# A message-passing layer on one core: the sums of a group made eight times side by side in place of four

## The chip, the cores and the metric

The kernel runs on one core of one Trainium2 chip. The metric is the device time of one execution in microseconds. A core has TensorE (PE, with its weight loads PEld), VectorE (DVE), ScalarE (ACT), GpSimd (POOL) and SyncE (SP), each with a queue of its own, and 16 DMA engines.

## The reference

The layer has 12500 nodes with 64 features and 212500 edges with 32 features, everything in float32. The edges are sorted by their target node.

```python
msg_in = concatenate([nodes[row], nodes[col], edge_features], axis=-1)
messages = relu(msg_in @ mW1 + mb1) @ mW2 + mb2
aggregated = segment_sum(messages, col, num_segments=12500)
upd_in = concatenate([nodes, aggregated], axis=-1)
u = relu(upd_in @ uW1 + ub1) @ uW2 + ub2
out = layernorm(nodes + u)          # over the 64 features, no scale
```

The hidden layer has 128 units. The kernel sums the hidden units over the edges of a node first and applies `mW2`, folded into the update's weights, afterwards.

## The kernel before, in words

**Groups.** The edges are cut into 554 groups (`G`) of three tiles of 128 edges. As they are sorted, the targets of a group lie in a window of 32 nodes (`W`). A group passes through three parts.

- `turn` (L318, L326): three gathers (`gather`, L132, indirect DMAs issued by POOL, 128 rows of 64 features each) have put the source nodes' rows beside a one-hot matrix of the edges' places in the window, which VectorE makes (L306), in one of 20 buffers `own_s`. PE transposes the three tiles (L318) and ACT copies them, 96 rows by 384 columns, into `own_st` (L326), where a DMA by SP has put the edge features. The copy also counts the edges of each node.
- `hidden` (L339, L349): three matmuls of `own_st` with the group's weights `own_wm` make the hidden units before relu, and ACT writes relu of them to `own_h`. Thirty-two rows of `own_wm` are the window's target nodes times their weights; they are made for four groups at a time (L285, L292, L297).
- `sums` (L363, L365): one small transpose brings the counts into a row. Three matmuls, one for each tile, have the hidden units as the stationary operand and the one-hot matrix as the moving one, and accumulate in PSUM the sums of the hidden units for each of the 32 nodes. VectorE adds them to `agg` (L374) and the counts to a row of `xc` (L375), at the window's place.

**The copies of the sums.** The one-hot matrix has 32 columns. The kernel before repeats it `TIMES` = 4 times along the moving operand with a broadcast, so that a matmul has 128 columns, and the sums stand four times side by side in the PSUM bank. Only the first copy is read.

**Steps.** One loop over `k` writes out the order for all engines. For the first 544 values a step on PE is the transposes of group k, the hidden units of group k - 2 and the sums of group k - 4, one after another, and only the last matmul of a step tells that it is done. Everything that follows the step waits for that: the copy L326, relu L349, the adds L374 and L375. Two sets of PSUM banks alternate between the steps, so a step waits for what read the step two before. VectorE makes the one-hot of group k + 1 before the adds of step k in its queue. For the last ten groups (`SHORT`) every part is a step of its own, and the sums of groups 540 to 543 already fall into that part.

**Gathers.** The gathers of group k + 16 stand in POOL's queue after step k. A gather waits until the copy L326 of the group 20 before it has read its buffer.

**Update.** Every 512 nodes whose edges are done are updated between the steps (L392 to L426): two matmuls with 512 columns, relu, four matmuls, the layer norm and a store.

If the edges were not sorted a second program would run; it does not run here.

Of the kernel before, what the change touches and what calls it, by code (L numbers as in the profile page):

```python
# [28 lines left out]
W = 32  # L29
TG = 3  # L30
GE = TG * P
G = (E + GE - 1) // GE
# [10 lines left out]
BITS = 16  # L43
NEAR_GROUPS = 24
SHORT = 10
TIMES = 4


def tiles_of(g):

    n = min(GE, E - g * GE)
    return [min(P, n - j * P) for j in range((n + P - 1) // P)]
# [43 lines left out]
def ordered(ctx: ExitStack, tc: tile.TileContext, a, own, ok):  # L96
# [21 lines left out]
    def after(first, *others):  # L118

        tc.declare_no_dep(first.ins, group="quiet", reason="waits for the last of a step")  # L120
        for i in others:
            tc.add_manual_dep(
                first.ins, i.ins.name,
                mybir.DependencyInfo(mybir.DependencyClass.Sync, mybir.DependencyReason.DATA),
                reason="the kernel's own rings",
            )
        return first
# [160 lines left out]
    def windows(b, wp, own_bank=True):  # L288


        xw, n = xws.pop(b)
        did = nc.tensor.matmul(wp[: n * W, :], xw[:, :n, :], w1b, start=True, stop=True)  # L292

        def copies():
            for i in range(n):
                g = b * SB + i
                c = nc.vector.tensor_copy(wm[g % NW][:W, :], wp[i * W : (i + 1) * W, :])  # L297
                after(c, *([did] if own_bank else []), *([hidden_by[g - NW]] if g >= NW else []))
                wm_by[g] = c

        return did, copies
# [57 lines left out]
    def sums(g, ps):  # L359
        h, s = own.h[g % NH], own.s[g % RING]  # L360
        sizes = tiles_of(g)
        sg = ps[:, 2, : (TIMES + 1) * W].rearrange("p (t w) -> p t w", w=W)
        did = [nc.tensor.transpose(sg[0:1, TIMES, :], counts[:W, g : g + 1], ident[:W, :W])]  # L363
        for j, p in enumerate(sizes):
            did.append(nc.tensor.matmul(  # L365
                sg[:, :TIMES, :], h[:p, j, :],
                s[:p, j, :W].unsqueeze(1).to_broadcast([p, TIMES, W]),
                start=j == 0, stop=j == len(sizes) - 1))

        def add(step):  # L370
            sums_by[g] = step
            at = bass.ds(starts.pop(g), W)
            return [
                after(nc.vector.tensor_tensor(agg[:, at], sg[:, 0, :], agg[:, at], ALU.add), step),  # L374
                after(nc.vector.tensor_tensor(xc[0:1, at], sg[0:1, TIMES, :], xc[0:1, at],  # L375
                                              ALU.add), step),
            ]

        return did, [*relu_by[g], copy_by[g]], add
# [53 lines left out]
    def step_update(g):  # L433
# [5 lines left out]
        elif now:  # L439
            got = now[1](now[0])  # L440
            now = [got, *now[2:]] if len(now) > 2 else []

    users = {part: [[], []] for part in (turn, hidden, sums)}

    def step(*work):
# [10 lines left out]
        for part, g, *_ in parts:  # L456
            if part is sums:
                for b in [b for b in xws if (b - 1) * SB <= g][:1]:
                    last, copies = windows(b, own.ps[g % 2][:, 2, (TIMES + 1) * W :][:, :H])
                    did.append(last)  # L460
# [18 lines left out]
    for k in range(G):  # L479
        if k < BITS:  # L480
            bit(k)
        if k % SB == 2:
            inputs(k // SB + 2)
        if k % SB == 1:
            places(k // SB + 1)
        onehot(k + 1)
        if k < G - SHORT:
            step((turn, k), *([(hidden, k - 2)] if k > 1 else []),
                 *([(sums, k - 4)] if k > 3 else []))
            made, summed = max(0, k - 1), max(0, k - 3)  # L490
        else:

            step((turn, k))
            for _ in range(2):
                if summed < made:
                    step((sums, summed))
                    summed += 1
            for _ in range(2):
                if made <= k:
                    step((hidden, made))  # L500
                    made += 1
        if k + AHEAD < G:
            gather(k + AHEAD)
# [332 lines left out]
```

## Time and profile before

| | |
|---|---|
| median of 8 runs | 2565.02 us (2561.79 to 2568.23) |
| the profiled execution | 2563.38 us |
| its span, first to last instruction | 2561.7 us |
| mean granted clock of TensorE | 0.771 of full speed |
| busy: PE, PEld, POOL | 1652.9, 1434.5, 1574.3 us |
| busy: DVE, ACT | 572.4, 542.0 us |
| granted clock, tenths, 40 slices | 9577777777877777877777877877777778777778 |

An engine's busy time counts each moment once, however many of its instructions overlap. The clock of a slice is the mean of what the throttle granted. "Idle before" is the time that an engine stood still ahead of a group of instructions, with what ended it. The chain is followed back from the last instruction, at each step to what released it.

### The profile page before, as it was taken

Reading aid. Unit: us, or ns where it says so; the run is one execution under the profiler, and the core shown is the slowest. Engines: PE = TensorE matmul, PEld = TensorE weight load, DVE = VectorE, ACT = ScalarE, POOL = GpSimd, SP = SyncE. Lnnn points to the kernel's source line nnn. Section 1 sums busy time; section 2 is a strip of 40 time slices with the busy share of each in tenths; the row PEclk is TensorE's granted clock in tenths of the full one; section 3 lists DMA queues with packets and bytes.
Section 4 is the critical chain, followed back from the end, with each engine's and each line's share of the span. In section 5 each row is a group of like instructions: output and inputs, shape, how many; then the busy total and the mean of one; then the engine's idle time right before and its main releaser. Section 6 shows DMA issues by size and latency. Waiting matters only on the chain.

```text
span 2561.7 us, 30668 instructions
## 1 busy us (share of the span) xinstructions
PE 1652.9 (65%) x9441; PEld 1434.5 (56%) x9441; DVE 572.4 (22%) x3191; ACT 542.0 (21%) x1715; POOL 1574.3 (61%) x1668
## 2 busy tenths in 40 slices
PE   1366666666676666766666666756667676666667
PEld 0355555555565555655565555655556565655565
DVE  4012122221221221222212222222222122122222
ACT  0122222222222222222222222222222222222222
POOL 7566666666666666666666666666666666666650
PEclk9577777777877877777877877778777878777778
DMA  4221111111111111111111111111111111111110
GB/s 89 45 48 39 34 37 36 35 36 38 34 39 32 39 39 31 39 34 37 39 34 37 36 35 36 37 37 36 38 34 39 32 39 39 32 36 37 36 36 12
DMA packets 73364, 96.05 MB, mean 37 GB/s; under 512 B 33451, under 2 KB 40842, under 8 KB 73194
## 3 DMA queue, kind: packets, MB, share of 16 engines
q0 software_dynamic: 53152, 54.51, 12.2%
q1 hardware_dynamic: 19128, 39.03, 5.4%
q8 instruction: 80, 1.31, 0.2%
q14 instruction: 90, 0.74, 0.1%
q10 hardware_dynamic: 914, 0.46, 0.1%
HBM read 90.58 MB, written 3.20 MB: 37 GB/s over the span
## 4 chain that ended last, share of the span: by engine, by line
PE 43%; another core or an unknown queue 31%; issue 14%; ACT 9%; DVE 2%; DMA 0%; DVEq 0%; SPq 0%; ACTq 0%
PE own_ps L365 17%; PE own_ps L339 12%; PE own_ps L318 7%; ACT own_st L326 5%; ACT own_h L349 5%; PE own_ps L363 2%; PE own_ps L292 1%; PE u_ps L405 1%; PE u_ps L392 1%; PE u_ps L393 1%; DVE mv L412 0%; DVE stats L411 0%; DMA dlc_i<-in_dst_cols 0%; DVE own_wm L297 0%
## 5 line engine op out<-in xcount | busy, mean ns | idle before, releaser
L132 POOL DMA_INDIRECT own_s<-in_x,src_sb x1661 | 1573.5, 947 | 912.4 <-issue 538.9
L318 PE MATMUL own_ps<-own_ident,own_s 128*96 128x128 f32 x1661 | 363.0, 340 | 792.8 <-issue 435.4
L318 PEld LDWEIGHTS own_ps<-own_ident,own_s 128*96 128x96 f32 x1661 | 227.4, 158 | 865.4 <-issue 477.0
L326 ACT ACTIVATE own_st<-own_ps 96x384 f32<-96x384 f32 x554 | 268.8, 485 | 1878.4 <-remote 873.3
L365 PE MATMUL own_ps<-own_s,own_h 128*128 128x128 f32 x3322 | 652.9, 345 | 3.2 <-issue 3.2
L339 PE MATMUL own_ps<-own_wm,own_st 128*128 128x128 f32 x3322 | 610.0, 335 | 1.2 <-DVE own_wm L297 1.2
L339 PEld LDWEIGHTS own_ps<-own_wm,own_st 128*128 128x128 f32 x3322 | 565.7, 251 | 4.7 <-DVE own_wm L297 1.6
L365 PEld LDWEIGHTS own_ps<-own_s,own_h 128*128 128x128 f32 x3322 | 530.5, 238 | 29.8 <-issue 2.5
L374 DVE TENSOR_TENSOR agg<-own_ps,agg 128x32 f32 x554 | 106.0, 191 | 1842.7 <-ACT own_h L349 1229.5
L349 ACT ACTIVATE own_h<-own_ps 128x384 f32<-128x384 f32 x553 | 264.2, 478 | 17.0 <-PE own_ps L339 13.1
L297 DVE COPY own_wm<-own_ps 32x128 f32<-32x128 f32 x550 | 155.1, 282 | 7.0 <-issue 1.0
L306 DVE TENSOR_TENSOR own_s<-iota,dlc 128x96 f32<-128x96 f32 x554 | 133.0, 241 | 4.7 <-issue 0.6
L363 PE MATMUL own_ps<-own_ident,own_counts 32*1 32x32 f32 x554 | 107.0, 193 | 4.0 <-ACT own_st L326 1.9
L326 ACT ACTIVATION_READ_ACCUMULATOR own_st<-own_ps 96x1 f32 x554 | 106.7, 193 | 0.0
L375 DVE TENSOR_TENSOR xc<-own_ps,xc 1x32 f32 x554 | 99.1, 179 | 15.2 <-PE u_ps L393 6.4
L363 PEld LDWEIGHTS own_ps<-own_ident,own_counts 32*1 32x1 f32 x554 | 41.1, 74 | 94.7 <-issue 49.1
L405 PE MATMUL u_ps<-u,u 128*128 128x64 f32 (+1 forms) x196 | 49.9, 406 | 28.5 <-issue 15.4
L405 PEld LDWEIGHTS u_ps<-u,u 128*128 128x128 f32 (+1 forms) x196 | 47.1, 324 | 31.9 <-issue 16.3
L285 DVE COPY xw<-xc 66x32 f32 x554 | 60.4, 175 | 3.0 <-issue 2.4
L292 PE MATMUL own_ps<-w1b,xw 66*128 66x128 f32 (+1 forms) x276 | 58.6, 296 | 0.0
L392 PE MATMUL u_ps<-agg,wc 128*128 128x512 f32 (+1 forms) x50 | 36.4, 820 | 28.1 <-issue 17.1
L292 PEld LDWEIGHTS own_ps<-w1b,xw 66*128 66x128 f32 (+1 forms) x276 | 47.0, 213 | 0.1
(58 smaller groups left out, 202.0 us busy)
## 6 DMA issues: line engine op xcount, KB each, us to landing
own_s<-in_x,src_sb POOLq DMA_INDIRECT x1661
own_st<-in_efT SPq DMA_DIRECT2D x138, 192.0 KB
xin<-in_x SPq DMA_DIRECT2D x24, 128.0 KB
out<-o SPq DMA_DIRECT2D x24, 128.0 KB
xc<-in_xT SPq DMA_DIRECT2D x12, 179.2 KB
dlc_i<-in_dst_cols SPq DMA_DIRECT2D x1, 831.0 KB
xc<-in_xT SPq DMA_DIRECT2D x4, 179.5 KB
src_sb<-in_src SPq DMA_DIRECT2D x13, 50.5 KB
```

Source lines behind the costliest of these rows:

```text
L132: nc.gpsimd.indirect_dma_start(out=s[:p, j, W:], out_offset=None, in_=x[:, :], in_offset=bass.IndirectOffsetOnAxis(ap=src_sb[:p, g * TG + ...
L292: did = nc.tensor.matmul(wp[: n * W, :], xw[:, :n, :], w1b, start=True, stop=True)
L297: c = nc.vector.tensor_copy(wm[g % NW][:W, :], wp[i * W : (i + 1) * W, :])
L306: places_by[g] = nc.vector.tensor_tensor(own.s[g % RING][:, :, :W], iota.unsqueeze(1).to_broadcast([P, TG, W]), dlc[:, g * TG : (g + 1) * ...
L318: nc.tensor.transpose(xt[:, j * P : j * P + p], s[:p, j, :], ident[:p, :p])
L326: nc.scalar.activation(t[: D + W, c : c + n], xt[:, :n], AF.Copy, accum_out=counts[:, g : g + 1]), step)
L339: nc.tensor.matmul(pre[:p, j, :], t[:, c + j * P : c + j * P + p], wm[g % NW], start=True, stop=True)
L349: relu_by[g] = [nc.scalar.activation(h, pre, AF.Relu)]
L363: did = [nc.tensor.transpose(sg[0:1, TIMES, :], counts[:W, g : g + 1], ident[:W, :W])]
L365: did.append(nc.tensor.matmul(sg[:, :TIMES, :], h[:p, j, :], s[:p, j, :W].unsqueeze(1).to_broadcast([p, TIMES, W]), start=j == 0, stop=j = ...
L374: after(nc.vector.tensor_tensor(agg[:, at], sg[:, 0, :], agg[:, at], ALU.add), step),
L405: nc.tensor.matmul(o_ps[:p, k], u[:, k:q:n], u2, start=True, stop=True)
```

## The change

`TIMES` becomes 8: the moving operand of the sums' matmuls has 256 columns and the sums stand eight times side by side. The last ten groups keep four copies (`FEW`). The transposed counts now stand behind eight copies in the bank. The number and the order of instructions on every engine are the same.

```diff
-TIMES = 4
+TIMES = 8
+FEW = 4
...
         sg = ps[:, 2, : (TIMES + 1) * W].rearrange("p (t w) -> p t w", w=W)
+        times = TIMES if g < G - SHORT else FEW
         did = [nc.tensor.transpose(sg[0:1, TIMES, :], counts[:W, g : g + 1], ident[:W, :W])]
         for j, p in enumerate(sizes):
             did.append(nc.tensor.matmul(
-                sg[:, :TIMES, :], h[:p, j, :],
-                s[:p, j, :W].unsqueeze(1).to_broadcast([p, TIMES, W]),
+                sg[:, :times, :], h[:p, j, :],
+                s[:p, j, :W].unsqueeze(1).to_broadcast([p, times, W]),
                 start=j == 0, stop=j == len(sizes) - 1))
```

## The prediction

> **What bounds the kernel now.** I read the page's groups first, then the chain, the waits, the timeline of an ordinary stretch and of the stretch in which the gathers have stopped, and last two windows of different clock.
>
> ```profile
> PE 1652.9 (65%) x9441; PEld 1434.5 (56%) x9441; DVE 572.4 (22%) x3191; ACT 542.0 (21%) x1715; POOL 1574.3 (61%) x1668
> L132 POOL DMA_INDIRECT own_s<-in_x,src_sb x1661 | 1573.5, 947 | 912.4 <-issue 538.9
> L365 PE MATMUL own_ps<-own_s,own_h 128*128 128x128 f32 x3322 | 652.9, 345 | 3.2 <-issue 3.2
> ```
>
> No engine is full. The sums are L365: 1661 matmuls, three for each group of three tiles, with two records each. POOL works 0.947 us on a gather and starts the next 1.25 us after the last when nothing stops it, so 1661 gathers need 2076 us. The rest of POOL's idle time is waiting, above all for L326 (363.9 us in the view of waits), since a gather may fill a buffer only when the group 20 before it was copied.
>
> ```profile
> PE 43%; another core or an unknown queue 31%; issue 14%; ACT 9%; DVE 2%; DMA 0%; DVEq 0%; SPq 0%; ACTq 0%
> PE own_ps L365 17%; PE own_ps L339 12%; PE own_ps L318 7%; ACT own_st L326 5%; ACT own_h L349 5%; PE own_ps L363 2%; PE own_ps L292 1%; PE u_ps L405 1%; PE u_ps L392 1%; PE u_ps L393 1%; DVE mv L412 0%; DVE stats L411 0%; DMA dlc_i<-in_dst_cols 0%; DVE own_wm L297 0%
> ```
>
> The 31%, 794 us, are time that no record explains. The timeline shows what it is. L326 copies the transposes of one step, in order, and waits for the last matmul of that step.
>
> ```profile
> 1013.60 0.85 PE L318 MATMUL own_ps<-own_ident,own_s 128*96 128x128 f32 x3
> 1015.19 0.94 PE L365 MATMUL own_ps<-own_s,own_h 128*128 128x128 f32 x6
> 1015.96 0.49 PE L318 MATMUL own_ps<-own_ident,own_s 128*96 128x128 f32 x3
> 1019.70 0.49 ACT L326 ACTIVATE own_st<-own_ps 96x384 f32<-96x384 f32 x1 [4.90 <-PE own_ps L292]
> 1021.27 0.84 PE L318 MATMUL own_ps<-own_ident,own_s 128*96 128x128 f32 x3 [2.94 <-ACT own_h L349]
> ...
> 2493.05 0.49 PE L318 MATMUL own_ps<-own_ident,own_s 128*96 128x128 f32 x3
> 2494.26 0.94 PE L365 MATMUL own_ps<-own_s,own_h 128*128 128x128 f32 x6
> 2495.23 0.49 ACT L326 ACTIVATE own_st<-own_ps 96x384 f32<-96x384 f32 x1 [1.02 <-PE own_ps L365]
> ```
>
> The step that starts at 1013.60 has its last record end at 1016.13, but its copy starts at 1019.70, 3.6 us later, and PE's step after next (1021.27) starts only after that. The step at 2493.05 ends at 2495.20 and is copied at 2495.23. Between these, one thing differs: POOL's last gather starts at 2486.5. Matching the copies with the triples of L318 in order over groups 20 to 535, I count 3.1 us on average from a step's recorded end to its copy, and about one step in four with less than 0.1 us. So while gathers run, most steps are seen as finished long after PE's records end. What holds them back the trace does not name.
>
> ```profile
> 2200.00:2300.00 100.00, 67.73 (x376) 59.30 (x376) 21.64 (x125) 22.26 (x71) 62.49 (x67) 0.72 0.17 35
> 1400.00:1500.00 100.00, 65.27 (x380) 55.62 (x381) 22.98 (x132) 22.68 (x72) 62.66 (x67) 0.83 0.18 37
> 2493.00:2505.00 12.00, 10.51 (x84) 9.35 (x83) 4.55 (x26) 5.05 (x16) 0.00 (x0) 1.00 0.06 16
> 1000.00:1012.00 12.00, 5.91 (x36) 4.92 (x35) 2.79 (x17) 2.76 (x9) 7.18 (x8) 0.78 0.19 39
> ```
>
> The first two windows hold 67 gathers each, with a granted clock of 0.72 and of 0.83: a PE that is 15% quicker did not make the groups come quicker. The last two show how the clock goes with PE's work: 1.00 at 10.51 us busy of 12 (88%), 0.78 at 49%.
>
> **The change, part by part.** Sums: groups 0 to 543 get a moving operand of 256 columns in place of 128. That is 544 x 3 x 2 = 3264 records. What a record of more columns costs is read from starts. At half clock the two 512-column records of L393 take from 222.52 to 224.22, 0.85 us each, and the three 128-column records of L318 after them to 224.86, 0.213 each: four times the columns, four times the time. So 256 columns take 0.427 us at half clock and 0.213 at full clock, where 128 took 0.213 and 0.11. Added: 3264 x 0.107 = 349 us if the clock were always full, 3264 x 0.213 = 695 us if always half, and at the mean clock of 0.771 3264 x 0.139 = 453 us.
>
> Page "TensorE: Matmul & The Clock Gate", section "Back-to-back issue gap", of the Trainium skill gives 134 cycles for 128 columns and 262 for 256 when warm, which would add an estimated 174 us in 3264 records. The trace has two passes in each record (0.11 us, not 0.056), and by the rows it is 349.
>
> Nothing else moves: the order of instructions on every engine is the same, no wait is added, the bank holds it (9 x 32 columns and 128 for the windows, 416 of 512), VectorE still adds 32 columns from the first copy, and the transposed count only lies further along. The last ten groups keep 128 columns. But the sums of groups 540 to 543 are made in the last part, where no gathers run: 24 records x 0.107 = 2.6 us with nothing to cover them.
>
> Clock: PE's 1652.9 us at 0.771 become (1652.9 + 453) x 0.771 = 1624 us of full-clock work. Busy share b = 1624 / (2562 c), which is 0.634 / c. A straight line through (0.645, 0.771) and the end row (0.88, 1.00) gives c = 0.771 + 0.97 (b - 0.645). Both hold at about c = 0.86 (b = 0.74). This is an estimate; its bounds are no change (0.771) and 1.00.
>
> The same page, section on the HAM clock gate, has the clock as half or full only, half after a window of some 3.4 us of idleness. If eight copies left no such window, the clock would be 1.00.
>
> What lies on the path: on the chain the PE lines other than L365 have 22%, 564 us. At 0.86 they shrink by 564 x (1 - 0.771/0.862) = 60 us. Half of that I count as gained, since the two windows show that a quicker PE is largely swallowed by the late completions: -30 us. The sums' own growth, 453 us at the old clock, 0.83 us in a group, I count at nothing beyond the 2.6 us: it ends before the copy would have started in the three steps of four that wait 0.1 to 10 us. If that cover is gone it costs what the rivals below say. The sum against the profiled execution (2563.4 us; span 2561.7 and 1.7 around it): 2563.4 - 30 + 2.6 = 2536. The median of the runs is 1.6 us above the profiled one, so I say 2537.
>
> **Rivals.** *The cover is missing where it counts (slower).* The steps that complete at once, one in four, are where PE's end is the completion. There 136 groups each get 0.83 us later: +113, less 30: 2648. The place is the copy L326 after these steps, which POOL waits for; it decides when POOL has used up the gathers that earlier copies allow. A step early in a run of gathers has some 2.5 us to spare (two more gathers), a step at its end none. For it: all of the 363.9 us of POOL's waiting for L326. Against it: the two windows. At its worst completion follows PE's end in every step. Then L365's 435 us on the chain become 435 x 2 x 0.771/0.862 = 778, +343, less 60: 2848. A single decisive price inside this is the clock staying at 0.77, when a half-clock step grows from 3.84 us (1009.97 to 1013.81) to 5.12, over the 4.5 us that a group has.
>
> *Nothing to be seen.* All of PE's time is covered, the clock's gain too: 2563 + 2.6 - 2, within 0.2%.
>
> *A larger gain.* A steadier PE lets copies come before POOL has run dry. A third of POOL's wait for L326 gone is -121: 2444. For it: three quarters of the steps are not at PE's speed now, so their pattern may shift. Against it: nothing in the change touches the gathers.
>
> *The change is not made as told.* Left out: the built program has 544 groups with 256 columns and ten with 128.
>
> **How the numbers follow.** Forecast (hidden, clock up): 0.46 with the larger gain, of which 0.06 lies below 2450. No difference, within 0.2% (5 us, about what a measurement of this kernel tells from none): 0.10. Slower: 0.44, of which 0.32 lies up to 2720 and 0.12 above, towards 2848. The range 2450 to 2720 leaves out 0.18. The forecast's own range is 2500 to 2560. Both signs hold most of the chance, and the point is that of the likeliest single case.
>
> **What would show it.** L365 at 345 ns mean now: records of about 450 to 480 ns, PE busy near 75%, a clock near 0.86. Right, if the mean distance from a step's end to L326 shrinks by about what the steps grow, and POOL's wait for L326 does not grow. Wrong on the cover, if L326 waits for L365 longer with L365's chain share near 30%. Wrong on the clock, if it stays below 0.80. The stretch after the last gather should be 3 us longer.

## The result: 2572.4 us, slightly slower

| | before | after |
|---|---|---|
| median | 2564.2 us (33 runs) | 2572.4 us (12 runs) |
| ratio | | 1.0034, 95% interval 1.0027 to 1.0042 |
| the profiled execution, its span | 2563.4, 2561.7 us | 2573.9, 2572.1 us |
| mean granted clock | 0.771 | 0.874 |

The change costs 8 us by the medians. In the experiments further on, two single executions of the kernel before took 3002.7 and 3002.9 us, at a granted clock of 1.00, where the others took 2101 to 2108 us; they are left out of the ratios there. The page of the profiled execution after, with the line of busy times, the two lines of the chain, and the groups that the forecast speaks of (busy time, mean ns of one, idle time before them):

```profile
PE 1862.5 (72%) x9441; PEld 1505.4 (59%) x9441; DVE 572.9 (22%) x3191; ACT 543.6 (21%) x1715; POOL 1573.5 (61%) x1668
...
PE 49%; another core or an unknown queue 25%; issue 14%; ACT 9%; DVE 2%; DMA 0%; ACTq 0%; DVEq 0%
PE own_ps L367 26%; PE own_ps L340 11%; PE own_ps L319 6%; ACT own_h L350 4%; ACT own_st L327 4%; PE u_ps L407 2%; PE own_ps L365 2%; PE own_ps L293 1%; PE u_ps L394 1%; PE u_ps L395 1%; ACT u L397 0%; DMA u1s<-in_uW 0%; DVE own_wm L298 0%; DVE mv L414 0%
...
L133 POOL DMA_INDIRECT own_s<-in_x,src_sb x1661 | 1572.7, 947 | 918.8 <-issue 546.5
L367 PE MATMUL own_ps<-own_s,own_h 128*128 128x256 f32 (+1 forms) x3322 | 1001.7, 444 | 0.0
L319 PE MATMUL own_ps<-own_ident,own_s 128*96 128x128 f32 x1661 | 315.1, 304 | 605.7 <-issue 282.8
...
L340 PE MATMUL own_ps<-own_wm,own_st 128*128 128x128 f32 x3322 | 533.7, 304 | 0.6 <-DVE own_wm L298 0.6
```

The transposes and the hidden units in the page of before:

```profile
L318 PE MATMUL own_ps<-own_ident,own_s 128*96 128x128 f32 x1661 | 363.0, 340 | 792.8 <-issue 435.4
...
L339 PE MATMUL own_ps<-own_wm,own_st 128*128 128x128 f32 x3322 | 610.0, 335 | 1.2 <-DVE own_wm L297 1.2
```

The line numbers have moved by one up to L350, and the sums are L367. Read against before: PE worked 209.6 us longer, and the span is only 10.4 us longer. The sums grew by 348.8 us (652.9 to 1001.7). The hidden units shrank by 76.3 (L339 610.0, L340 533.7) and the transposes by 47.9 (363.0 to 315.1), although their number and shape are the same: they run at a higher clock. On the chain the sums rose from 17% to 26%, and the time that no record explains fell from 31% to 25%. POOL's work and its idle time are almost the same.

In the timeline after, one stretch with gathers and one behind the last gather, the steps of PE and their copies L327:

```profile
1000.45 0.49 PE L319 MATMUL own_ps<-own_ident,own_s 128*96 128x128 f32 x3
...
1001.66 1.56 PE L367 MATMUL own_ps<-own_s,own_h 128*128 128x256 f32 x6
...
1006.91 0.49 ACT L327 ACTIVATE own_st<-own_ps 96x384 f32<-96x384 f32 x1 [2.00 <-remote]
...
1007.09 0.51 PE L319 MATMUL own_ps<-own_ident,own_s 128*96 128x128 f32 x3 [3.87 <-issue]
...
2500.23 1.56 PE L367 MATMUL own_ps<-own_s,own_h 128*128 128x256 f32 x6
...
2501.83 0.49 ACT L327 ACTIVATE own_st<-own_ps 96x384 f32<-96x384 f32 x1 [1.65 <-PE own_ps L367]
```

The step that starts at 1000.45 ends at 1003.22, and its copy comes at 1006.91, 3.7 us later. Behind the last gather (2492.2) the sums end at 2501.79 and the copy comes 0.04 us later. So the late completions of before are still there. Counted over groups 20 to 535, in the same way as before, a step of PE lasts 3.29 us in place of 2.88, and the copy comes 2.51 us after its end in place of 3.09. From the start of a step to its copy it is 5.80 us in place of 5.97.

One more count from the two traces says what sets the pace. When the transposes of a group start, POOL has started the gathers of 18.4 groups more on average (18.4 after the change too), nearly the 20 that the ring holds. So in these runs the steps hold back the gathers, and not the other way round.

POOL's wait for the copies in the view of waits (us in total, times, longest), before and after, and then two windows of 100 us of the run after, with the busy time of PE, PEld, DVE, ACT and POOL (instructions behind each), the granted clock, the share of DMA and GB/s:

```profile
POOL own_s L132 <- ACT own_st L326: 363.9, 136, 9.9
```

```profile
POOL own_s L133 <- ACT own_st L327: 362.7, 137, 9.1
```

```profile
2200.00:2300.00 100.00, 75.13 (x388) 61.06 (x387) 21.07 (x121) 21.34 (x68) 64.09 (x68) 0.89 0.18 38
1400.00:1500.00 100.00, 72.89 (x365) 58.17 (x365) 22.64 (x129) 21.80 (x71) 62.57 (x67) 0.88 0.18 37
```

POOL waits for the copies as long as before (363.9, now 362.7). The first window had 67 gathers at a clock of 0.72 and has 68 at 0.89: the pace did not follow the clock.

The 10 us of the two profiled executions lie in two places. The last gather starts 5.7 us later (2486.5, now 2492.2). From there to the end it takes 80.0 us in place of 75.1.

### The profile page after: what moved, and what is told of

Read it like the earlier page. It is cut to its first block, busy times and chain, and to the rows that moved or that the text cites. A ratio compares the mean times of both kernels' runs of the same rounds, so it can differ in the third digit from the quotient of the medians.

```text
span 2572.1 us, 30668 instructions
## 1 busy us (share of the span) xinstructions
PE 1862.5 (72%) x9441; PEld 1505.4 (59%) x9441; DVE 572.9 (22%) x3191; ACT 543.6 (21%) x1715; POOL 1573.5 (61%) x1668
## 4 chain that ended last, share of the span: by engine, by line
PE 49%; another core or an unknown queue 25%; issue 14%; ACT 9%; DVE 2%; DMA 0%; ACTq 0%; DVEq 0%
PE own_ps L367 26%; PE own_ps L340 11%; PE own_ps L319 6%; ACT own_h L350 4%; ACT own_st L327 4%; PE u_ps L407 2%; PE own_ps L365 2%; PE own_ps L293 1%; PE u_ps L394 1%; PE u_ps L395 1%; ACT u L397 0%; DMA u1s<-in_uW 0%; DVE own_wm L298 0%; DVE mv L414 0%
## 5 line engine op out<-in xcount | busy, mean ns | idle before, releaser
L367 PE MATMUL own_ps<-own_s,own_h 128*128 128x256 f32 (+1 forms) x3322 | 1001.7, 444 | 0.0
L319 PE MATMUL own_ps<-own_ident,own_s 128*96 128x128 f32 x1661 | 315.1, 304 | 605.7 <-issue 282.8
L367 PEld LDWEIGHTS own_ps<-own_s,own_h 128*128 128x128 f32 x3322 | 672.2, 218 | 111.2 <-issue 0.4
L327 ACT ACTIVATE own_st<-own_ps 96x384 f32<-96x384 f32 x554 | 269.0, 486 | 1876.6 <-remote 784.3
L319 PEld LDWEIGHTS own_ps<-own_ident,own_s 128*96 128x96 f32 x1661 | 205.2, 143 | 735.7 <-issue 347.6
L340 PE MATMUL own_ps<-own_wm,own_st 128*128 128x128 f32 x3322 | 533.7, 304 | 0.6 <-DVE own_wm L298 0.6
L340 PEld LDWEIGHTS own_ps<-own_wm,own_st 128*128 128x128 f32 x3322 | 485.8, 220 | 3.0 <-DVE own_wm L298 1.1
L350 ACT ACTIVATE own_h<-own_ps 128x384 f32<-128x384 f32 x553 | 264.1, 478 | 18.6 <-PE own_ps L340 18.6
L365 PE MATMUL own_ps<-own_ident,own_counts 32*1 32x32 f32 x554 | 105.0, 190 | 4.3 <-ACT own_st L327 1.9
L327 ACT ACTIVATION_READ_ACCUMULATOR own_st<-own_ps 96x1 f32 x554 | 106.6, 192 | 0.0
L365 PEld LDWEIGHTS own_ps<-own_ident,own_counts 32*1 32x1 f32 x554 | 41.1, 74 | 84.1 <-issue 26.2
L293 PEld LDWEIGHTS own_ps<-w1b,xw 66*128 66x128 f32 (+1 forms) x276 | 55.8, 203 | 9.0
L394 PE MATMUL u_ps<-agg,wc 128*128 128x512 f32 (+1 forms) x50 | 28.4, 651 | 15.8 <-DVE agg L376 8.8
```

The costliest lines, as they stand in the source:

```text
L319: nc.tensor.transpose(xt[:, j * P : j * P + p], s[:p, j, :], ident[:p, :p])
L327: nc.scalar.activation(t[: D + W, c : c + n], xt[:, :n], AF.Copy, accum_out=counts[:, g : g + 1]), step)
L340: nc.tensor.matmul(pre[:p, j, :], t[:, c + j * P : c + j * P + p], wm[g % NW], start=True, stop=True)
L350: relu_by[g] = [nc.scalar.activation(h, pre, AF.Relu)]
L367: did.append(nc.tensor.matmul(sg[:, :times, :], h[:p, j, :], s[:p, j, :W].unsqueeze(1).to_broadcast([p, times, W]), start=j == 0, stop=j = ...
```

## The experiments

They ran later, on four chips, on each of which the median of the kernel before is 2103 to 2105 us. The record names these four, but not the chip of the runs above. "The first chip" below means that chip in the state that it was in then, and "other chips" means these four in theirs. Ratios are to the kernel before on the same chip.

**What the other chips show.** The kernel before and the changed one, unedited:

> The kernel before, for its profile beside the runs of this call. If the chip that runs it shows what the first runs showed, it takes about 2564 us and the copy of a step (L326) starts 3.1 us on average after the step's last PE record; if it is one where the gathers alone set the pace, it takes about 2105 us and the copy starts under 0.1 us after it. Theory A (the late completions belong to the chip or its state, not to the program) allows both; theory B (they belong to the program) allows only the first.

> The changed kernel again. Theory A (where the gathers set the pace at 1.25 us each, the longer steps are hidden whole): a ratio of 1.000 to 1.001 where before takes 2105 us, all of the loss in the tail of the last ten groups; 1.003 again where it takes 2564 us. Theory B (the eight copies cost something wherever a step ends, whatever paces the kernel): 1.003 on both.

Before took 2102.4 us. Changed: 2103.49 against 2103.49 us, ratio 0.9998 (0.9989 to 1.0007). The page of the kernel before on such a chip, with its line of busy times, its chain by engine and by line, and its groups of gathers, transposes, sums and hidden units:

```profile
PE 1418.9 (68%) x9441; PEld 1206.8 (57%) x9441; DVE 573.8 (27%) x3191; ACT 553.5 (26%) x1715; POOL 1571.9 (75%) x1668
...
DMA 45%; POOL 31%; issue 16%; PE 6%; ACT 1%; DVE 1%; POOLq 0%; DVEq 0%; SPq 0%; ACTq 0%
DMA own_s<-in_x,src_sb 45%; POOL own_s L132 31%; PE own_ps L365 2%; PE own_ps L339 2%; PE own_ps L318 1%; ACT own_h L349 1%; PE u_ps L405 0%; POOLq L132 0%; ACT own_st L326 0%; PE own_ps L363 0%; PE u_ps L392 0%; PE u_ps L393 0%; DVE mv L412 0%; DMA xin<-in_x 0%; DVE stats L411 0%
L132 POOL DMA_INDIRECT own_s<-in_x,src_sb x1661 | 1571.1, 946 | 507.2 <-issue 374.9
L318 PE MATMUL own_ps<-own_ident,own_s 128*96 128x128 f32 x1661 | 302.0, 295 | 634.9 <-DVE own_s L306 243.6
...
L365 PE MATMUL own_ps<-own_s,own_h 128*128 128x128 f32 x3322 | 570.1, 313 | 0.0
L339 PE MATMUL own_ps<-own_wm,own_st 128*128 128x128 f32 x3322 | 500.3, 291 | 1.2 <-DVE own_wm L297 1.2
```

The part "another core or an unknown queue", 31% of the chain on the first chip, is not there, and 76% of the chain is gathers: POOL's work on them and their landing. POOL's idle time is 507 us in place of 912, and no copy is among its main causes. When a group's transposes start, POOL is only 1.6 groups ahead. A copy L326 starts 0.04 us on average after its step's end, where the first chip had 3.1. So the gathers set the pace here. Theory A holds as far as it can be tried: the same program runs without late completions, so they belong to the chip or its state, and where the gathers set the pace the copies are free. The page of the changed kernel there, with its transposes:

```profile
PE 1643.6 (78%) x9441; PEld 1310.5 (62%) x9441; DVE 590.6 (28%) x3191; ACT 555.4 (26%) x1715; POOL 1570.6 (75%) x1668
...
L319 PE MATMUL own_ps<-own_ident,own_s 128*96 128x128 f32 x1661 | 280.1, 278 | 411.3 <-DMA own_s<-in_x,src_sb 189.8
```

PE does 225 us more than the 1418.9 us of before, and its idle time ahead of the transposes falls by 224 us (634.9 to 411.3): the longer sums fill time in which PE stood still, and none of it shows in the time. Two repeats agree:

> The changed kernel once more. Two chips so far took 2103 to 2105 us for the kernel before and showed no late completions; the first measurements had 2564 us and a ratio of 1.003. Where before takes 2103 to 2105 us I expect 0.999 to 1.001 by the theory that the gathers set the pace; where it takes 2564 us, 1.003 as at first.

> The changed kernel beside the kernel before. Theory A (what makes it lose 8 us is the late completions of the first chip): 0.999 to 1.001 where before takes 2103 to 2105 us, 1.003 where it takes 2564 us. Theory B (the tail of the last ten groups costs 4 to 5 us on every chip): 1.002 everywhere.

0.9998 (0.9988 to 1.0007) and 0.9997 (0.9987 to 1.0007).

**More copies, and none in the end.**

```diff
-TIMES = 8
+TIMES = 11
```

> Eleven copies of the sums (352 columns) for groups 0 to 543, four for the last ten. Cover theory: still covered, since a full-clock step is about 2.14 + 6 x 0.187 = 3.26 us against 4.5 us in a group; 2570 to 2590 us, what is added comes in the stretch after the last gather. Balance rival: the clock can rise only from 0.87 to some 0.92, the added 261 us of full-clock work are not paid back: PE +190 us, by its chain share +90: about 2660 us.

> Eleven copies up to group 543. Where before takes 2564 us it says how the late completions take up a longer step. Theory A (a step's end is swallowed by a completion that comes at its own time): within 15 us of the changed kernel, the distance from a step's end to L327 shrinking again by what the step grows (about 0.4 us). Theory B (part of the steps is paced by PE itself): another 10 to 60 us. Where before takes 2103 to 2105 us: 1.000 to 1.001, as at first.

1.0006 (0.9997 to 1.0015) and 1.0010 (1.0000 to 1.0019). The sums have 1121.8 us there, and PE is busy 90% of the span; the cover holds even then, to within 0.2%.

```diff
-        times = TIMES if g < G - SHORT else FEW
+        times = TIMES if g < 530 else FEW
```

> Eight copies for groups 0 to 529 only, four for the last 24, whose sums are made about when the gathers end. If the 8 us that the change lost lie in the stretch after the last gather (79.97 against 75.13 us in the profiles), some 5 us come back: ratio to before 1.000 to 1.002. If they lie in the main part, the ratio stays at 1.003.

> Eight copies only for groups 0 to 529, so that every step after the last gather is as before. Where before takes 2564 us: if the changed kernel's loss of 8 us lies half in the stretch behind the last gather, 1.0015; if all of it lies in the stretch of the gathers, 1.003; if the longer steps made the last gather no later, 1.000. Where before takes 2103 to 2105 us: 0.999 to 1.000.

0.9992 (0.9983 to 1.0001) and 0.9995 (0.9985 to 1.0004): it cannot be told from the kernel before, so no version here beats it.

**One copy.** The edit against the changed kernel:

```diff
-TIMES = 8
+TIMES = 4
+MAIN = 1
...
-        times = TIMES if g < G - SHORT else FEW
+        times = MAIN if g < G - SHORT else FEW
```

> One copy of the sums (32 columns) for groups 0 to 543, four for the last ten; all else as before. Cover theory: the groups' pace in the main part is set by the gathers and by the late completions, so taking PE work away changes nothing: 2550 to 2570 us, PE busy down to some 1450 us or less, the clock down towards 0.70, the distance from a step's end to L326's copy up from 3.1 us. Balance rival (in the change, the eight copies cost time on the path and the higher clock gives as much back): PE's time matters by its share of the chain, 43%; PE loses some 200 us net of the lower clock, so about 2480 us.

> One copy, 32 columns. It took 2173 us at a clock of 0.526 where before takes 2105 us, with PE busy 97% of the span. Theory A (32 columns leave the granted clock at half whatever the chip): the same again, 2165 to 2180 us. Theory B (that clock was the chip's): the clock at 0.8 or more and about 2105 us. Where before takes 2564 us: over 2600 us.

2172.8 us, ratio 1.0321 (1.0303 to 1.0339), and 2133.6 us in a single run on the same chip later. The page of the first, with its slices of granted clock and its groups of sums and hidden units:

```profile
PE 2123.6 (97%) x9441; PEld 1897.2 (87%) x9441; DVE 577.2 (26%) x3191; ACT 555.4 (25%) x1715; POOL 1571.0 (72%) x1668
...
PEclk9555555555555555555555555555555555555557
...
L341 PE MATMUL own_ps<-own_wm,own_st 128*128 128x128 f32 x3322 | 814.0, 417 | 0.0
L368 PE MATMUL own_ps<-own_s,own_h 128*128 128x32 f32 (+1 forms) x3322 | 812.1, 400 | 0.0
```

The clock stays at half (0.526, then 0.551) although PE is busy 97% of the span. The hidden units, which the edit does not touch, take 417 ns each; they take 291 in the kernel before on such a chip. PE has become the bound, and its completions are prompt (0.04 us). The forecast's straight line from busy share to clock has no place for this: with 32 columns a PE whose longest pause is 0.56 us (from 100 us on to the last gather) is still at half clock. So the four copies of the kernel before are worth having: with them even the sums are shorter, 570.1 us in place of 812.1, although they have four times the columns. The repeat stayed 31 us below the 2165 to 2180 us that were expected; it is slower than before all the same, at nearly the same clock.

**The cost of the copies where nothing covers them.** In both kernels:

```diff
     def gather(g):
         s = own.s[g % RING]
+        if g >= RING:
+            loads[g] = []
+            return
```

> The kernel before with only the first 20 groups' gathers; later groups use what lies in the buffers (gathers of groups 20 to 553 are left out). If the gathers hold the steps' completions back: the copies L326 start within 0.1 us of the step's end in nearly every step, the clock near 1.0, groups come at about 2.3 us as between 2493 and 2505 us in the trace of before, 1350 to 1500 us in all. If the delay is PE's or ACT's own: a distance of 2 to 3 us stays and the groups take about 4 us: some 2300 us.

> Four copies, gathers of the first 20 groups only. Where before takes 2103 to 2105 us: 1462 us as before. Where it takes 2564 us: theory A (gathers make completions late): 1462 us too, the copy within 0.1 us of each step's end; theory B (the chip's completions are late by themselves): well over 1700 us.

> Eight copies, and only the first 20 groups' gathers are issued: the later groups compute on the rows that lie in the ring. It shows what the copies cost where no gather covers them. The same with four copies took 1462 us with PE busy 1250 us at a clock of 0.994. Theory A (the cost is on PE's stream and nothing else hides it): 534 groups of 3 tiles (some 3270 records) by 0.105 to 0.11 us, 345 to 360 us more, about 1810 us. Theory B (half of it lies in idle time of PE between steps): about 1640 us.

Four copies took 1462.1 and 1464.6 us, eight, on another of the chips, 1714.1. From the pages of the first with four and of the one with eight, PE's line, the sums and the transposes (in kernels so edited the lines stand elsewhere):

```profile
PE 1249.9 (86%) x9441; PEld 1107.5 (76%) x9441; DVE 562.8 (39%) x3191; ACT 554.4 (38%) x1715; POOL 58.4 (4%) x67
...
L368 PE MATMUL own_ps<-own_s,own_h 128*128 128x128 f32 x3322 | 519.6, 293 | 0.0
...
L321 PE MATMUL own_ps<-own_ident,own_s 128*96 128x128 f32 x1661 | 276.8, 276 | 162.9 <-ACT own_h L352 144.8
```

```profile
PE 1585.2 (93%) x9441; PEld 1326.8 (77%) x9441; DVE 573.1 (33%) x3191; ACT 555.3 (32%) x1715; POOL 58.4 (3%) x67
...
L370 PE MATMUL own_ps<-own_s,own_h 128*128 128x256 f32 (+1 forms) x3322 | 860.8, 396 | 0.0
...
L322 PE MATMUL own_ps<-own_ident,own_s 128*96 128x128 f32 x1661 | 276.6, 276 | 79.4 <-issue 61.3
```

The sums grew by 341.2 us at a clock of 0.99 and more; the forecast had 349 for full clock. The time grew by 252 us: PE's busy time grew by 335 us, and 84 us of that went into waits of PE ahead of the transposes, which fell from 163 to 79 us. Neither theory had that share right (345 to 360, or 180).

**Gathers uncoupled from the steps.** The gathers of group 20 and later write four spare tiles and wait for no copy. The steps compute on what lies in the ring.

```diff
+        if g >= RING:
+            loads[g] = []
+            free[g] = [
+                nc.gpsimd.indirect_dma_start(
+                    out=spare[g % 4][:p, j, :], out_offset=None, in_=x[:, :],
...
+                for j, p in enumerate(tiles_of(g))
+            ]
...
+            return
```

> Four copies; from group 20 on the gathers write four spare tiles in turn, so that POOL waits for no copy and PE for no gather, and the steps compute on the rows that lie in the ring. It shows what each of the two costs alone. Theory A (POOL's gathers are the pace, 1.25 us each when nothing holds them): 1661 by 1.25 and some 25 us at the end, about 2100 us, the same as before where before takes 2105 us, and 2100 to 2150 us where before takes 2564 us, since the late completions then hold nothing. Theory B (the completions are late because gathers run, and PE's own steps are then the pace): 4.6 us a step, about 2500 us where before takes 2564 us.

> Four copies, the gathers of group 20 and later written to four spare tiles without waiting for a copy, the steps computing on the rows that lie in the ring. Where before takes 2564 us: if the late completions come from gathers that run, they stay late and the steps take 4 to 4.6 us each (2250 to 2560 us in all); if they come from the loop between copy and gather, they are prompt and POOL ends last at 2090 us. Where before takes 2103 to 2105 us: 2091 as in the last call.

> Eight copies, the gathers of group 20 and later written to four spare tiles without waiting for a copy, the steps computing on the rows that lie in the ring. With four copies it took 2090 us, and the copy of step 535 came at about two thirds of the span. I expect 2090 us again, since POOL ends last either way, and the steps 0.47 us longer each as without gathers (1714 less 1462 us over 534 groups): the sums that were 28 of 40 slices take some 33. If gathers slow PE's records, more than that. Where before takes 2564 us: steps of about 4.5 us with late completions, or the same as elsewhere.

2090.8 and 2090.0 us with four copies, 2092.5 with eight. PE's busy tenths in 40 slices, four copies and then eight:

```profile
PE   2888888888888888888888888887000000000000
```

```profile
PE   2999999999999999999999999999999950000000
```

The steps are over after 28 and after 33 slices, and POOL goes on alone. Between the copies of groups 20 and 500 a group took 2.54 us with four copies and 3.00 with eight; without gathers it was 2.53 and 2.99. So gathers that run beside PE slow neither its records nor its completions on these chips, and 0.46 us is the price of the copies in a group at full clock.

**PE's own steps set the pace, with pauses.** No run fell on a chip with late completions, so I made a loop of steps in which PE has pauses and the gathers are not the bound. In both kernels one set of PSUM banks serves all steps:

```diff
-            ps, old = own.ps[g % 2], users[part][g % 2]
+            ps, old = own.ps[0], users[part][0]
...
-            users[part][g % 2] = follow(did[-1])
+            users[part][0] = follow(did[-1])
...
```

> Four copies and one set of PSUM banks for all steps: a step of PE (2.2 us without waits for gathers) is followed by the copy and relu of that step, 0.49 + 0.19 + 0.47 us and some 0.1 us of hand-over, before the next starts. About 3.5 us a step and 3.9 us with the windows and updates: 544 steps, 2050 to 2250 us, near the gathers' own 2076 us. PE stands still a third of each step, so the clock should be 0.75 to 0.9.

> Eight copies and one set of banks. The forecast's theory, with the cover taken away: the sums add 0.47 us a step at full clock (1714 less 1462 us over 534 groups) and the clock rises by some 0.09, which shrinks the other PE work of 1.6 us a step by 0.15: 0.3 us net, 534 steps, 120 to 180 us slower than with four copies if PE's steps set the pace in both. Rival, that a raised clock pays for the copies where PE is in the loop: within 20 us of four copies, or quicker. Third, that the gathers cover it: both within 30 us of 2105.

Four copies: 2784.3 us (2778.3 to 2802.2, 4 runs), clock 0.753. Eight: 2920.4 us (2907.0 to 2929.9, 4 runs), clock 0.883. By chance nearly the two clocks of the first chip. The time with four copies lies 534 us above the upper end of what I expected: I had written the step at full clock (2.2 us; it lasts 3.03) and had no room in the sum for waits behind the updates. The difference of 136 us is in the range of the first theory. The pages, four copies and then eight, with PE, the gathers, the transposes, the sums and the hidden units:

```profile
PE 1796.3 (64%) x9441; PEld 1514.1 (54%) x9441; DVE 574.1 (21%) x3191; ACT 557.3 (20%) x1715; POOL 1576.1 (57%) x1668
...
L132 POOL DMA_INDIRECT own_s<-in_x,src_sb x1661 | 1575.3, 948 | 1076.2 <-ACT own_st L326 642.9
L318 PE MATMUL own_ps<-own_ident,own_s 128*96 128x128 f32 x1661 | 367.9, 344 | 930.5 <-ACT own_h L349 538.6
...
L365 PE MATMUL own_ps<-own_s,own_h 128*128 128x128 f32 x3322 | 711.7, 369 | 0.0
...
L339 PE MATMUL own_ps<-own_wm,own_st 128*128 128x128 f32 x3322 | 646.5, 349 | 7.8 <-DVE xc L375 3.8
```

```profile
PE 1920.6 (66%) x9441; PEld 1481.0 (51%) x9441; DVE 574.0 (20%) x3191; ACT 556.2 (19%) x1715; POOL 1568.6 (54%) x1668
...
L367 PE MATMUL own_ps<-own_s,own_h 128*128 128x256 f32 (+1 forms) x3322 | 1031.5, 455 | 0.0
L319 PE MATMUL own_ps<-own_ident,own_s 128*96 128x128 f32 x1661 | 304.9, 296 | 930.3 <-ACT own_h L350 538.5
...
L340 PE MATMUL own_ps<-own_wm,own_st 128*128 128x128 f32 x3322 | 524.0, 300 | 7.9 <-DVE xc L377 3.8
```

PE's idle time ahead of the transposes is the same in both, 930 us, most of it waiting for relu, which follows the copy of the step before. So what PE's records add is what the time adds:

| us | first chip | one set of banks |
|---|---|---|
| sums | +348.8 | +319.8 |
| hidden units | -76.3 | -122.5 |
| transposes | -47.9 | -63.0 |
| the rest of PE | -15.0 | -10.0 |
| PE busy | +209.6 | +124.3 |
| span | +10.4 | +123.7 |

Where PE is in the loop, the higher clock gives back 195 us and the copies take 320. Both count, whole, and the net is a loss. On the first chip 5% of the net shows.

This pair also says something of the late completions. POOL waits here for copies for 643 us, more than on the first chip, is 19.4 groups ahead of the transposes on average (there 18.4), and runs in bursts of 3, 6, 9 and 12 gathers as it does there. The clock, 0.753, is as low as there. The timeline with four copies, the sums of one step and its copy:

```profile
1010.27 0.94 PE L365 MATMUL own_ps<-own_s,own_h 128*128 128x128 f32 x6
```

```profile
1011.24 0.49 ACT L326 ACTIVATE own_st<-own_ps 96x384 f32<-96x384 f32 x1 [2.64 <-PE own_ps L365]
```

The sums end at 1011.21 and the copy starts 0.03 us later; the mean is 0.04. So on these chips neither waiting for copies nor such bursts nor a low clock make the completions late.

## Why the prediction was wrong

**Right.** *The cost of 256 columns.* 341 us at full clock were measured without gathers, 349 forecast. On the first chip the records became 444 ns; I had said 450 to 480. The estimate of 174 us from the Trainium skill, page "TensorE: Matmul & The Clock Gate", section "Back-to-back issue gap", is about half of the 341. *The clock.* 0.86 forecast, 0.874 measured, with PE at 72% where I had 74%. There is luck in it: for the kernel before on the other chips, with PE at 68%, the same line gives 0.80, and 0.93 was measured. The same page's section on the HAM clock gate has the clock as half or full only, half after some 3.4 us of idleness. The clock's records in the traces of these runs have half or full and nothing between, as it says. The 3.4 us do not come out: between 100 us and the last gather the longest pause of PE is 3.40 us in both runs with one set of banks and 0.56 us with one copy, and the mean clocks are 0.753, 0.883 and 0.526. A clock of 1.00 did not come on the first chip; it came, as 0.996, with eight copies on the other chips, where the longest pause is 1.47 us. *The cover.* The steps became 0.41 us longer and the distance to the copy 0.58 us shorter, and POOL's wait for copies did not grow. The rival with the cover missing, 2648 us and more, is out on that chip; what it describes is the pair with one set of banks.

**Wrong: the gain of 30 us.** The step that failed is "Half of that I count as gained", the -30 in the sum 2563.4 - 30 + 2.6. I had taken 60 us for the other PE lines that shrink with the clock, and at the same time counted the growth of the sums at nothing. But everything behind a step waits for its last matmul alone. The transposes, the hidden units and the sums of a step stand one after another on PE, so a copy cannot see the first two become quicker unless the step as a whole does. It became longer, 2.88 to 3.29 us, and PE's busy time rose by 210 us. Either the step is covered, and then both terms are zero, or it is not, and then both count and the sum is a loss, as the pair with one set of banks has it (-195 and +320). My two windows at 0.72 and 0.83 with equal gathers had said the first, and I weakened that to a half where it called for a zero. The 60 us were also added up short: the printed chain has 25% for the PE lines other than L365, not 22%, since the updates' lines belong to them, which would make some 68 us. That does not change the step that failed. Without the -30 the sum is 2566 in the profiled execution's terms, 0.1% above before: nothing to be seen, or slower.

**Undersized: the stretch behind the last gather.** I had 2.6 us for the 24 records of groups 540 to 543. The copies of 19 groups still lie behind the last gather (20 after the change), so the sums of groups 531 to 543 are made there too: 13 groups, 78 records, 78 x 0.107 = 8.3 us at full clock. The stretch grew by 4.8 us; the clock there was 0.92 in place of 0.86, which may have taken the rest back, but no run tries that. With 4.8 and no gain the sum is 2563.4 + 4.8 = 2568.2, against 2573.9 measured.

**What stays open.** The other 5.7 us of the profiled pair, by which the last gather starts later. They are 0.23% of the stretch and 3% of the growth of PE, and may be the part of the steps that complete at once; no run tells that. They did not build up evenly: the same gather of the two traces starts 3.2 us earlier after the change (at about the 300th), 1.9 later (the 1000th), 8.8 later (the 1400th) and 5.7 later (the last). Why completions are late on the first chip is open as well. The time is the same for both kernels on the four other chips and the lateness is absent there, so the program alone does not make it, and PE with pauses, POOL in bursts and gathers that run beside PE have been shown not to make it there. Nothing was tried on the first chip in its state, and chip and state cannot be told apart. So that the late completions are what took up the 0.41 us of a step on the first chip is read from its two traces, and not shown by an experiment.

## What to carry to other kernels

A step that is released by its last instruction has one length. When one part of it grows and another shrinks, add them up first and ask only then whether the sum is covered; a gain from one part and cover for the other cannot both be had. Extra work to raise the clock pays only where the clock's gain on the rest is larger than the work: here 195 us against 320 from four copies to eight, while from one copy to four even the sums themselves became shorter. And when a stretch without the usual cover is costed, count from the trace which instructions still lie in it, not from the loop's bounds.

## What the runs showed of the hardware

- The same program takes 2564 us in the runs of the result and 2103 to 2105 us on four chips later. In the first, PE's steps are seen as finished 3.1 us late on average while gathers run, and 0.04 us late behind the last gather; on the four chips they are 0.04 us late throughout.
- With one copy, 32 moving columns in the sums, the granted clock stays at 0.53 to 0.55 with PE busy 97%; with 128 columns it is 0.93 at 68%, with 256 and 352 columns 0.996 and 0.997. So the clock does not follow PE's busy time in the profile alone.
- The clock goes down without long pauses: with one set of banks and four copies no pause of PE between 100 us and the last gather is over 3.40 us, and the mean clock is 0.753.
